# Reordering channels so that one matrix serves the group norms, and projecting q and k together: a four-layer fp32 convolution stack on one core

## The chip, the cores and the metric

The kernel runs on one core of one Trainium2 chip. The metric is device time in microseconds (us) of one execution; lower is better. The kernel before has a median of 4973.22 us over 3 runs (4967.2 to 4978.35). All data and all arithmetic are fp32.

## The reference, cut to what matters

The input x is 4 x 384 x 64 x 64 (batch, channels, height, width). Four layers follow, each as `x = x + layer(group_norm(x))`. A group norm has 32 groups, so 12 neighbouring channels share one mean and one variance per batch.

```python
def _gn(v, G=32, eps=1e-5):
    g = v.reshape(B_, G, C_ // G, H_, W_)
    m = jnp.mean(g, axis=(2, 3, 4), keepdims=True)
    s = jnp.var(g, axis=(2, 3, 4), keepdims=True)
    return ((g - m) / jnp.sqrt(s + eps)).reshape(v.shape)
...
# layer 0: attention on the first 96 channels, then a projection of all 384
xn = layer_norm_over_channels(x[:, :96])
qkv = bn(einsum(w_qkv, xn))              # 16 q, 16 k, 96 v channels
attn = softmax(q^T k * 16**-0.5)         # 4096 x 4096 per batch
y = bn(einsum(w_proj, relu(concat([v attn^T, x[:, 96:]]))))
```

Layer 1 is a 1x1 convolution, a filter over 8x8 patches in the frequency domain, a 3x3 depthwise convolution, a gated gelu and a 1x1 convolution. Layer 2 has 5x5 and 3x3 depthwise convolutions, gates, and an MLP from 384 to 768 to 384 channels with batch norms. Layer 3 is a 7x7 depthwise convolution whose kernels depend on the data. Which order the channels lie in matters to none of this as long as every weight that is indexed by channel lies in the same order, and the output is put back.

## The kernel before, in words

The 384 channels lie as three blocks `j` of 128 partitions. Channel c sits in block c // 128 on partition c % 128.

**Group norm.** Every norm starts from a mean and a variance per channel, kept as `[128, 3, ...]` (partition, block). The sum over a group goes across partitions, so it is a matmul with a constant matrix. Groups of 12 don't divide 128, and a group can straddle two blocks. So there are seven constant matrices `group[i, j]`, |i - j| < 2, loaded at the start (L238), and one sum over groups takes seven matmuls (`of_group` within `norm_of_groups`, L355 to L384, with one moving column each; `over_groups`, L561, with four). `norm_of_groups` sums twice: first the means (`gn_pg`), which VectorE copies to `gn_gm`; then VectorE forms (mean - group mean)^2 + variance (`gn_d`, L376 to L378), which is summed as `gn_pv`; ScalarE reads that from PSUM and takes Ln and Exp for the inverse root (`gn_r`). It is called 12 times: for x of each batch (`x_norm`), for the output of layer 0 (end of `attention`, L767), and for the output of layer 1 (end of `layer1`, L846). `group_means` and `factors` (layer 3) use `over_groups` once each.

**q, k, v.** `qkv` (L614) works through eight blocks of 512 pixels. Of each it centers 96 channels with a matmul (`ln_s`), gets the variance with another (`ln_v`), normalises to `ln_xn`, and then projects. `wq4` holds the 16 query columns four times, at columns 0, 32, 64 and 96 (`q_m`, L633), since the scores use four row groups of 32 partitions side by side. `wk4` holds the key columns four times as well (`k_m`, L639). ScalarE copies `q_m` to `q[i]` in one instruction (L634); a DMA on SP's queue then writes a row of shifts into it (L635). VectorE takes from `k_m` four pieces of 32 partitions x 128 columns, group g from partitions 32 g (L641). Four small matmuls make `v_m` (L645).

**The order of the work.** The first phase (`phase_a`) runs the attention of batch b and, beside it, other work: the norm of batch b+1's x, layer 1 of batch b-1, and the qkv of batch b+1. `side_by_side` (L529) draws pieces of the other work after each of the 64 attention steps, in proportion to estimated costs that the pieces yield. The final order on each engine, the semaphores and the PSUM slots come from the framework's scheduler. In this phase the PSUM tiles made with `pm` (tag "m") share two banks: `q_m`, `k_m`, `v_m`, `ln_s`, `ln_v`, `gn_pg`, `gn_pv`, and the tiles of layers 0 and 1. The scores have one tile of four banks, the attention output has two banks.

An attention step is four matmuls of scores on row groups (`sc_s`, L715), two Exp instructions on ScalarE (`probs`, L723), and four matmuls with v (`av`, L752). A matmul of the code becomes two instructions on TensorE.

The later phases are the depthwise convolutions of layer 2 (`phase_b`), its MLP (`phase_ef`), and layer 3 (`phase_g`).

Of the kernel before, what the change touches and what calls it, by code (L numbers as in the profile page):

```python
# [21 lines left out]
F32 = mybir.dt.float32  # L22
AF = mybir.ActivationFunctionType
ALU = mybir.AluOpType
AX = mybir.AxisListType

B, C, H, W = 4, 384, 64, 64
N = H * W
NJ = 3
P = 128  # L30
PD = 96
# [41 lines left out]
def _constants():  # L73
    parts = {}
    parts["ident"] = np.eye(P)
    center = np.zeros((P, PD))
    center[:PD] = np.eye(PD) - 1.0 / PD
    parts["center"] = center
    parts["mean96"] = np.full((P, PD), 1.0 / PD)
    group = np.arange(C) // (C // 32)  # L80
    same = (group[:, None] == group[None, :]) / (C // 32)
    for i in range(NJ):
        for j in range(NJ):
            if abs(i - j) < 2:
                parts[f"group{i}{j}"] = same[i * P : (i + 1) * P, j * P : (j + 1) * P]
    basis, pick = _fourier()

    inv = np.zeros((2, 64, 8, 2, 8))
    for p in range(2):
        inv[p, :, :, p, :] = basis.reshape(64, 8, 8)  # L90
    inv = inv.reshape(P, P)
    parts["to_coef"] = inv.T
    parts["to_pos"] = inv
    pick_t = np.zeros((P, P))
    pick_t[:40] = np.concatenate([pick.T, pick.T], axis=1)
    parts["pick"] = pick_t
    parts["mean384"] = np.full((P, P), 1.0 / C)

    e, x = np.arange(P) // W, np.arange(P) % W
    near = np.abs(x[:, None] - x[None, :]) <= 3  # L100
    parts["band7"] = near[:, 0:W]
    parts["cols7"] = near & (e[:, None] == e[None, :])
    parts["same32"] = np.tile(np.eye(32), (4, 4))
    net = np.zeros((P, 2 * P))
    net[0, :P] = 1.0
    net[1, P:] = 1.0
    net[2, P:] = -1.0
    parts["net"] = net
    at = 0
    for k, v in parts.items():  # L110
        _CONST_COLS[k] = (at, at + v.shape[1])
        at += v.shape[1]
    return np.concatenate(list(parts.values()), axis=1).astype(np.float32)

_HID = np.concatenate([np.arange(0, 128), np.arange(192, 320), np.arange(128, 192), np.arange(320, 384)])


def _cols(v):  # L120
# [38 lines left out]


def _layout(i):
    vec = {}
    for k in ("bn2_g", "bn2_b", "bn2_m", "bn2_v"):
        vec[k] = _cols(i[f"L0_conv_{k}"])
# [62 lines left out]
class _Builder:  # L227
    def __init__(self, ctx, tc, ins, out):
        self.ctx, self.tc, self.nc = ctx, tc, tc.nc
        self.ins, self.out = ins, out  # L230
        nc = self.nc
        self.keep = ctx.enter_context(tc.tile_pool(name="keep", bufs=1))
        self.small = ctx.enter_context(tc.tile_pool(name="small", bufs=2))
        self.dram = ctx.enter_context(tc.tile_pool(name="dram", bufs=1, space=bass.MemoryType.DRAM))
        self.vecs = self.keep.tile([P, ins["vecs"].shape[1]], F32, tag="vecs", name="vecs")
        nc.sync.dma_start(self.vecs, ins["vecs"])
        self.ident = self.const(self.keep, "ident")
        self.group = {  # L238
            (i, j): self.const(self.keep, f"group{i}{j}") for i in range(NJ) for j in range(NJ) if abs(i - j) < 2
        }  # L240
        self.eps = self.keep.tile([P, 1], F32, tag="eps", name="eps")
        nc.gpsimd.memset(self.eps, EPS)
        self.scratch = {
            k: [[self.dram.tile([P, N], F32, tag=f"{k}{b}{j}", name=f"{k}_{b}_{j}") for j in range(NJ)] for b in range(B)]
            for k in ("x2",)
        }

        self.tok = self.dram.tile([UNITS, B, 32, N], F32, tag="tok", name="tok")

        self.wx, self.h2 = (  # L250
            [self.dram.tile([P, NJ, N], F32, tag=f"{k}{b}", name=f"{k}_{b}") for b in range(B)] for k in ("wx", "h2")
        )


        self.rest = self.dram.tile([P, 32, B, P], F32, tag="rest", name="rest")
        self.raw = [self.dram.tile([P, P, P], F32, tag=f"raw{j}", name=f"raw_{j}") for j in range(NJ - 1)]
        self.shifts = [self.dram.tile([4, N], F32, tag=f"shift{b}", name=f"shift_{b}") for b in range(B)]

        self.xa, self.x1 = (
            [self.dram.tile([P, NJ, N], F32, tag=f"{k}{b}", name=f"{k}_{b}") for b in range(B)] for k in ("xa", "x1")  # L260
        )

        self.d53 = [
            [self.dram.tile([32, B, 32, P], F32, tag=f"d{i}{u}", name=f"d_{i}_{u}") for u in range(UNITS)]
            for i in range(2)
        ]
        self.hidden = [self.dram.tile([6, P, N], F32, tag=f"hid{b}", name=f"hid_{b}") for b in range(B)]

        self.norm2 = self.keep.tile([P, 3, NJ, B], F32, tag="norm2", name="norm2")
        self.r2, self.n2, self.p2 = (self.norm2[:, i] for i in range(3))  # L270
        self.mvt_ = self.keep.tile([P, 2, NJ, B], F32, tag="mvt", name="mvt")
        self.mvt = self.mvt_.rearrange("p k j b -> p j b k")
# [79 lines left out]
        a, c = self.bn_scale_shift(name, mv[:, 0:1], mv[:, 1:2], g, b)  # L352
        nc.scalar.activation(out, z, func, bias=c, scale=a)

    def norm_of_groups(self, mv, beside=False):  # L355


        nc = self.nc

        def of_group(name, src):  # L360
            out = self.pm(name)
            for j in range(NJ):
                near = [i for i in range(NJ) if abs(i - j) < 2]
                for i in near:
                    nc.tensor.matmul(
                        out[:, j : j + 1], lhsT=self.group[i, j], rhs=src(i), start=i == near[0], stop=i == near[-1]
                    )
            return out

        pg = of_group("gn_pg", lambda i: mv[:, i, 0:1])  # L370
        gm = self.sm([P, NJ], "gn_gm", 3)
        nc.vector.tensor_copy(gm, pg[:, 0:NJ])
        d = self.sm([P, NJ], "gn_d")

        mean = pg[:, 0:NJ] if beside else gm
        nc.vector.tensor_sub(d, mv[:, :, 0], mean)  # L376
        nc.vector.tensor_mul(d, d, d)
        nc.vector.tensor_add(d, d, mv[:, :, 1])  # L378
        pv = of_group("gn_pv", lambda i: d[:, i : i + 1])
        r = self.sm([P, NJ], "gn_r", 3)  # L380
        self.rsqrt(r, pv[:, 0:NJ])
        n = self.sm([P, NJ], "gn_n", 3)
        nc.vector.scalar_tensor_tensor(n, mean, -1.0, r, ALU.mult, ALU.mult)
        return r, gm, n, mv  # L384


    def qkv_weights(self, pool):
# [3 lines left out]
        nc = self.nc  # L391
# [24 lines left out]
        for g in range(4):  # L416
            nc.vector.tensor_copy(self.wq4[:, g, 1:17], wt[:, 0:16])
            nc.vector.tensor_copy(self.wk4[:, g, 1:17], wt[:, 16:32])
        nc.vector.tensor_copy(self.wv[:, 0:PD], wt[:, 32:P])
        self.score_bound(pool, wt)  # L420

    def score_bound(self, pool, wt):
# [191 lines left out]
    def qkv(self, b, q, k4, vt):  # L614
        nc = self.nc
# [7 lines left out]
        for i in range(8):  # L623
# [5 lines left out]
                yield 1.0  # L629
            xa = xn[i]  # L630
            q[i] = self.big.tile([P, 512], F32, tag="q", name="q", bufs=9)
            m = self.pm("q_m")
            nc.tensor.matmul(m, lhsT=self.wq4.rearrange("p g d -> p (g d)"), rhs=xa, start=True, stop=True)  # L633
            nc.scalar.copy(q[i], m)  # L634
            nc.sync.dma_start(  # L635
                q[i].rearrange("(g d) n -> g d n", g=4)[:, 0], self.shifts[b][:, i * 512 : (i + 1) * 512]
            )
            m = self.pm("k_m")
            nc.tensor.matmul(m, lhsT=self.wk4.rearrange("p g d -> p (g d)"), rhs=xa, start=True, stop=True)  # L639
            for g in range(4):  # L640
                nc.vector.tensor_copy(k4[32 * g : 32 * g + 32, i], m[32 * g : 32 * g + 32, g * P : (g + 1) * P])  # L641
            m = self.pm("v_m")
            mv = m.rearrange("p (c d) -> p c d", d=P)
            for c in range(4):
# [906 lines left out]
    def group_means(self):  # L1551

        nc = self.nc
        m = self.over_groups("gn_pg", self.mean2)
        nc.vector.tensor_copy(self.gm, m)
        for i, k in enumerate((-6.0, -7.0, 2.0)):
            nc.vector.tensor_scalar(self.off[:, :, :, i], self.gm, k, None, ALU.mult)
        nc.gpsimd.memset(self.s_s, 1.0)
        nc.vector.tensor_scalar(self.s_b, self.gm, -1.0, None, ALU.mult)

    def over_groups(self, name, v):

        m = self.pm(name)[:, 0 : NJ * B].rearrange("p (j b) -> p j b", b=B)
        for j in range(NJ):
            near = [i for i in range(NJ) if abs(i - j) < 2]
            for i in near:
                self.nc.tensor.matmul(
                    m[:, j], lhsT=self.group[i, j], rhs=v[:, i], start=i == near[0], stop=i == near[-1]
                )
        return m  # L1570

    def factors(self):

        nc = self.nc
# [5 lines left out]
        sq = tile_of("g_sq")  # L1580
        nc.vector.tensor_mul(sq, avg, avg)
        nc.vector.scalar_tensor_tensor(d, d, 1.0 / N, sq, ALU.mult, ALU.add)
        pv = self.over_groups("gn_pv", d)
        r = tile_of("g_r")
        self.rsqrt(r, pv)
        nc.vector.tensor_mul(avg, avg, r)
# [299 lines left out]
```

## Time and profile before

| | |
|---|---|
| median, 3 runs | 4973.22 us (4967.2 to 4978.35) |
| profiled execution, span of its instructions (the page gives no other time of it) | 4964.9 us |
| TensorE (PE) busy | 4552.7 us, 92%, 17665 matmul instructions |
| VectorE (DVE) busy | 2769.8 us, 56%, 4438 |
| ScalarE (ACT) busy | 2136.4 us, 43%, 2873 |
| GpSimd (POOL) busy | 777.5 us, 16%, 593 |
| mean granted TensorE clock | 0.962 |
| attention phase with its neighbours | about 62 to 2300 us |
| rest of layer 1, then layer 2's convolutions | about 2300 to 3170 us |
| layer 2's MLP | about 3195 to 4195 us |
| layer 3 | about 4200 to 4965 us |

"Busy" is the time in which an engine executes something. It is an average over stages. The row of tenths shows the span in 40 slices. A timeline line has start and duration in us, engine, line, operation, output and inputs, the number of instructions merged, and in brackets the idle time before it with what ended it. PEld is the load of the stationary operand, which runs beside the matmul before it.

### The profile page before, as it was taken

What the parts mean: (1) busy time and instruction counts of PE and PEld (TensorE: products, weight loads), DVE (VectorE), ACT (ScalarE), POOL (GpSimd) and SP (SyncE); (2) the same over time, 40 slices, a digit from 0 to 9 for tenths busy, and PEclk for the clock granted to TensorE, in tenths of its full rate; (3) what the DMA queues carried; (4) which work ended last, traced back from release to release, by engine and by line L of the source; (5) the groups of instructions that cost most, each with busy time, mean ns of one, the idle gap of its engine ahead of it and who ended that gap; (6) DMA issues with size and microseconds to landing.
All of it is one profiled execution on the core that took longest, in us unless ns stands there. A gap on an engine that the chain in (4) does not pass through costs nothing.

```text
span 4964.9 us, 47732 instructions
## 1 busy us (share of the span) xinstructions
PE 4552.7 (92%) x17665; PEld 2564.5 (52%) x17665; DVE 2769.8 (56%) x4438; ACT 2136.4 (43%) x2873; POOL 777.5 (16%) x593
## 2 busy tenths in 40 slices
PE   5999999999999999998989999699999998677988
PEld 2343444434443344444557888444444443577888
DVE  5322465644666445555867778655531112667898
ACT  4444344454444444444435666411123333764321
POOL 1000000000000000000025555100000001125554
PEclk9999999999999999998989999799999999699999
DMA  5210211211111111112338999776664443896776
GB/s 169 73 47 30 85 54 55 72 56 39 64 64 51 55 45 58 58 57 78 120 122 276 291 292 292 250 278 256 256 245 157 153 152 132 316 343 203 239 255 227
DMA packets 346710, 752.64 MB, mean 152 GB/s; under 512 B 22779, under 2 KB 173158, under 8 KB 337510
## 3 DMA queue, kind: packets, MB, share of 16 engines
q1 hardware_dynamic: 280728, 475.46, 30.1%
q0 software_dynamic: 32640, 151.28, 7.9%
q10 hardware_dynamic: 33102, 122.77, 6.3%
q8 instruction: 143, 2.34, 0.2%
q14 instruction: 97, 0.79, 0.0%
HBM read 447.16 MB, written 302.25 MB: 151 GB/s over the span
## 4 chain that ended last, share of the span: by engine, by line
PE 45%; DVE 9%; DMA 4%; ACT 3%; issue 3%; POOL 1%; SPq 0%; ACTq 0%; DVEq 0%; POOLq 0%
PE h_s L1380 10%; PE h_m L1432 10%; PE conv_m L1156 9%; PE av L752 3%; PE t_m L871 2%; PE conv_m L1757 2%; DVE acc L948 2%; DMA wmix<-in_mix_t 1%; DMA g_h<-h 1%; PE out_m L966 1%; PE proj_m L785 1%; PE sc_s L715 1%; DVE toep L1744 1%; PE taps_m L941 1%; DVE toep L1137 1%
## 5 line engine op out<-in xcount | busy, mean ns | idle before, releaser
L752 PE MATMUL av<-probs,vt 128*128 128x512 f32 x2048 | 965.6, 607 | 0.0
L723 ACT ACTIVATE probs<-sc_s 128x1024 f32<-128x1024 f32 x512 | 500.9, 1021 | 789.8 <-PE av L752 783.7
L752 PEld LDWEIGHTS av<-probs,vt 128*128 128x128 f32 x2048 | 371.7, 192 | 468.1 <-issue 461.0
L1156 PE MATMUL conv_m<-toep,z 128*128 128x256 f32 x2304 | 519.4, 385 | 10.6 <-DVE toep L1137 5.1
L948 DVE SCALAR_TENSOR_TENSOR acc<-band,vecs,acc 128x512 f32<-128x512 f32 x708 | 496.9, 747 | 45.7 <-POOL band L909 39.9
L1432 PE MATMUL h_m<-f_h,cm_w_t 128*128 128x512 f32 x1152 | 496.7, 595 | 8.7 <-ACT f_h L1422 8.7
L1156 PEld LDWEIGHTS conv_m<-toep,z 128*128 128x128 f32 x2304 | 439.4, 193 | 71.0 <-DVE z L1089 4.9
L1757 PE MATMUL conv_m<-toep,z 128*128 128x128 f32 x3072 | 392.8, 286 | 42.1 <-DVE toep L1744 19.2
L1757 PEld LDWEIGHTS conv_m<-toep,z 128*128 128x128 f32 x3072 | 378.7, 202 | 44.4 <-POOL toep L1744 18.2
L1380 PE MATMUL h_s<-e_tok,cm_w_t 128*128 128x512 f32 x768 | 363.4, 596 | 5.5 <-DVE e_tok L1365 5.5
L1137 POOL TENSOR_TENSOR toep<-w,band 128x1536 f32<-128x1536 f32 x94 | 324.0, 3447 | 278.0 <-PE conv_m L1156 232.0
L1432 PEld LDWEIGHTS h_m<-f_h,cm_w_t 128*128 128x128 f32 x1152 | 220.0, 191 | 285.4 <-issue 273.3
L715 PE MATMUL sc_s<-q,k 32*128 32x512 f32 x2048 | 296.3, 647 | 21.9 <-ACT probs L723 21.4
L1440 DVE BATCH_NORM_STATS2 h_st<-f_h 128x6 f32<-128x512 f32 x96 | 66.4, 694 | 429.1 <-ACT f_h L1439 429.1
L871 PE MATMUL t_m<-w_in_t,xb 128*128 128x384 f32 x768 | 276.7, 495 | 3.4 <-DVE coef L888 2.1
L1387 ACT COPY e_h<-h_s 128x1024 f32<-128x1024 f32 x96 | 97.2, 1012 | 401.5 <-PE h_s L1380 401.5
L785 PE MATMUL proj_m<-xm,w_proj_t 128*128 128x512 f32 x576 | 265.2, 599 | 4.6 <-DVE xm L738 3.5
L792 DVE SCALAR_TENSOR_TENSOR x_res<-proj_m,bn_c,x_res 128x512 f32<-128x512 f32 x96 | 71.8, 748 | 319.0 <-PE proj_m L785 315.9
L1380 PEld LDWEIGHTS h_s<-e_tok,cm_w_t 128*128 128x128 f32 x768 | 147.0, 192 | 189.5 <-issue 183.2
L1389 DVE BATCH_NORM_STATS2 h_st<-e_h 128x6 f32<-128x512 f32 x192 | 123.4, 685 | 202.8 <-ACT e_h L1387 202.8
L871 PEld LDWEIGHTS t_m<-w_in_t,xb 128*128 128x128 f32 x768 | 142.9, 192 | 139.0 <-issue 59.3
L1380 PE MATMUL h_s<-z,cm_w_t 128*128 128x512 f32 x384 | 196.2, 593 | 0.0
(380 smaller groups left out, 6206.2 us busy)
## 6 DMA issues: line engine op xcount, KB each, us to landing
d<-d_o ACTq DMA_DIRECT2D x96, 512.0 KB
c_d<-d SPq DMA_DIRECT2D x96, 512.0 KB
hid<-e_h ACTq DMA_DIRECT2D x16, 3072.0 KB
f_h<-hid SPq DMA_DIRECT2D x16, 3072.0 KB
x_in<-in_x SPq DMA_DIRECT2D x96, 256.0 KB
x_res<-in_x SPq DMA_DIRECT2D x32, 768.0 KB
xa<-x_res POOLq DMA_DIRECT2D x32, 768.0 KB, 3.9
xa_in<-xa SPq DMA_DIRECT2D x32, 768.0 KB
```

The source lines that it names most:

```text
L715: nc.tensor.matmul(s[:, g], lhsT=k4[32 * g : 32 * g + 32, c], rhs=q[i][32 * g : 32 * g + 32], start=True, stop=True,)
L723: nc.scalar.activation(p[:, h * 1024 : (h + 1) * 1024], s[:, 2 * h : 2 * h + 2].rearrange("p a b -> p (a b)"), AF.Exp, scale=0.25,)
L752: nc.tensor.matmul(av, lhsT=vt[:, 4 * c + v, :], rhs=p[:, v * 512 : (v + 1) * 512], start=c == 0 and v == 0, stop=c == 7 and v == 3,)
L785: nc.tensor.matmul(m, lhsT=self.w_proj[:, j, o * P : (o + 1) * P], rhs=xm[:, j], start=j == 0, stop=j == NJ - 1,)
L871: nc.tensor.matmul(m[:, 0:C], lhsT=xb[:, j], rhs=self.w_in[:, j, :], start=j == 0, stop=j == NJ - 1,)
L948: nc.vector.scalar_tensor_tensor(out, src(j, k), w, done, ALU.mult, ALU.add)
L1137: eng.tensor_tensor(t, self.w53[:, at : at + 192].rearrange("p (m n) -> p m n", n=8).unsqueeze(2).to_broadcast([P, 24, 8, 8]), band.rearra ...
L1156: nc.tensor.matmul(m[:, c * 256 : (c + 1) * 256], lhsT=self.z_[:, at : at + P], rhs=t[:, 12 * c + 4 * i : 12 * c + 4 * i + 4].rearrange("p ...
L1380: nc.tensor.matmul(s[:, v, :], lhsT=w1[:, j, o * P : (o + 1) * P], rhs=t[j][:, v * 512 : (v + 1) * 512], start=j == 0, stop=j == NJ - 1,)
L1389: nc.vector.bn_stats(st[:, o, 8 * b + 2 * i + v, :], h[:, o, v * 512 : (v + 1) * 512])
L1432: nc.tensor.matmul(m, lhsT=w2[:, o, j * P : (j + 1) * P], rhs=h[:, o, v * 512 : (v + 1) * 512], start=o == 0, stop=o == 5,)
L1757: nc.tensor.matmul(m[:, ch * P : (ch + 1) * P], lhsT=self.z_[:, at : at + P], rhs=t[:, 8 * c + 2 * i : 8 * c + 2 * i + 2].rearrange("p m a ...
```

## The change

The channels are permuted on the host. Block j now holds, on its partitions 0 to 95, eight whole groups (channels 0 to 95, 192 to 287 and 288 to 383), and on partitions 96 to 127 the j-th third of each of the eight groups of channels 96 to 191, four channels of each. Then one matrix `group` describes every block: twelve neighbouring partitions belong together below 96, four above. The first 96 channels stay on block 0's first 96 partitions, where the attention wants them. All weights indexed by channel are permuted on the host, and so is the output.

One sum over groups is now one matmul with all blocks as moving columns, into an `m` of PSUM. VectorE then copies partitions 0 to 95, adds the three blocks for partitions 96 to 127, and copies that sum to all three blocks.

For q and k, `wqk` has the query columns at 0, 32 and 64 and the key columns at 96. One matmul gives `qk_m`. ScalarE copies partitions 0 to 95 to q, and with a second instruction partitions 64 to 95 to q's partitions 96 to 127. VectorE takes all four pieces of k from partitions 96 to 127.

```diff
-        self.group = {
-            (i, j): self.const(self.keep, f"group{i}{j}") for i in range(NJ) for j in range(NJ) if abs(i - j) < 2
-        }
+        self.group = self.const(self.keep, "group")
...
+    def of_groups(self, name, v):
+        nc = self.nc
+        n = v.shape[2]
+        m = self.pm(name)[:, 0 : NJ * n].rearrange("p (j n) -> p j n", n=n)
+        nc.tensor.matmul(m, lhsT=self.group, rhs=v, start=True, stop=True)
+        out = self.sm([P, NJ, n], f"{name}_{n}", 3)
+        nc.vector.tensor_copy(out[0:PD], m[0:PD])
+        s = self.sm([P, n], f"{name}_{n}s")
+        nc.vector.tensor_reduce(s[PD:P], m[PD:P].rearrange("p j n -> p n j"), AX.X, ALU.add)
+        nc.vector.tensor_copy(out[PD:P], s[PD:P].unsqueeze(1).to_broadcast([P - PD, NJ, n]))
+        return out
...
-        pg = of_group("gn_pg", lambda i: mv[:, i, 0:1])
-        gm = self.sm([P, NJ], "gn_gm", 3)
-        nc.vector.tensor_copy(gm, pg[:, 0:NJ])
+        gm = self.of_groups("gn_pg", mv[:, :, 0:1])[:, :, 0]
...
-        pv = of_group("gn_pv", lambda i: d[:, i : i + 1])
+        pv = self.of_groups("gn_pv", d)[:, :, 0]
         r = self.sm([P, NJ], "gn_r", 3)
-        self.rsqrt(r, pv[:, 0:NJ])
+        self.rsqrt(r, pv)
...
+        self.wqk = pool.tile([PD + 1, 4, 32], F32, tag="wqk", name="wqk")
+        nc.vector.tensor_copy(self.wqk[:, 0:3], self.wq4[:, 0:3])
+        nc.vector.tensor_copy(self.wqk[:, 3], self.wk4[:, 3])
...
-            m = self.pm("q_m")
-            nc.tensor.matmul(m, lhsT=self.wq4.rearrange("p g d -> p (g d)"), rhs=xa, start=True, stop=True)
-            nc.scalar.copy(q[i], m)
+            m = self.pm("qk_m")
+            nc.tensor.matmul(m, lhsT=self.wqk.rearrange("p g d -> p (g d)"), rhs=xa, start=True, stop=True)
+            nc.scalar.copy(q[i][0:96], m[0:96])
+            nc.scalar.copy(q[i][96:128], m[64:96])
...
-            m = self.pm("k_m")
-            nc.tensor.matmul(m, lhsT=self.wk4.rearrange("p g d -> p (g d)"), rhs=xa, start=True, stop=True)
             for g in range(4):
-                nc.vector.tensor_copy(k4[32 * g : 32 * g + 32, i], m[32 * g : 32 * g + 32, g * P : (g + 1) * P])
+                nc.vector.tensor_copy(k4[32 * g : 32 * g + 32, i], m[96:128, g * P : (g + 1) * P])
...
-        m = self.over_groups("gn_pg", self.mean2)
+        m = self.of_groups("g_pg", self.mean2)
...
-        pv = self.over_groups("gn_pv", d)
+        pv = self.of_groups("g_pv", d)
```

The rest of the diff is on the host: the permutation `_ORDER`, the list of weights it applies to, and its inverse on the output.

## The prediction

> **What bounds the kernel now.** I read the row of busy tenths first. From the second slice to the nineteenth (one slice is 124 us, so to about 2300 us) TensorE is at 9, and VectorE, ScalarE and DMA are not.
>
> ```profile
> PE   5999999999999999998989999699999998677988
> DVE  5322465644666445555867778655531112667898
> ACT  4444344454444444444435666411123333764321
> ```
>
> Everything that the change removes lies in this stretch, except the start and two sums in layer 3. A busy TensorE need not be the limit, so I read the chain of waits of a piece of it. From 1760 to 1790 us it holds TensorE alone, back to back: 14 `av` instructions in 6.01 us, 0.429 us each.
>
> ```profile
> 1767.24 1.07 PE sc_s L715 x8
> 1768.31 0.86 PE back_m L896 x6
> 1769.18 6.01 PE av L752 x14
> ```
>
> The engine's waits between 600 and 900 us come to 3.6 us in 300. So there a microsecond taken off TensorE is one taken off the time. The start is different. Of 60 to 140 us TensorE idles about 20, and the timeline shows why:
>
> ```profile
> 95.60 0.68 ACT L314 ACTIVATE ln_rs<-ln_v,eps 96x512 f32<-96x512 f32 x1
> 96.33 1.13 PE L639 MATMUL k_m<-ln_xn,wk 97*128 97x512 f32 x2 [1.35 <-ACT ln_rs L314]
> 98.13 0.56 ACT L634 COPY q<-q_m 128x512 f32<-128x512 f32 x1
> 98.74 1.16 PE L645 MATMUL v_m<-wv,ln_xn 97*128 97x128 f32 x8 [0.42 <-ACT q L634]
> 100.19 1.07 PE L589 MATMUL ln_s<-ln_x,center 96*96 96x512 f32 x2 [0.29 <-DVE k L641]
> ```
>
> Each tile of the two-bank pool waits until the tile two before it is read: `k_m` for `ln_v`, `v_m` for `q_m`, the next `ln_s` for `k_m`. ScalarE's strict order (Ln, table, Exp, then the q copy) sets the beat, about 10 us a block.
>
> **The norms**, from the timeline, once inside attention and once where attention ends:
>
> ```profile
> 1740.36 0.16 DVE L372 COPY gn_gm<-gn_pg 128x3 f32<-128x3 f32 x1 [2.15 <-PE gn_pg L365]
> 1740.56 0.16 DVE L376 TENSOR_TENSOR gn_d<-gn_mv,gn_gm 128x3 f32<-128x3 f32 x1
> 1741.17 1.72 PE L365 MATMUL gn_pv<-gn_d,group 128*128 128x1 f32 x14
> 2280.45 2.56 PE L365 MATMUL gn_pv<-gn_d,group 128*128 128x1 f32 x14 [0.84 <-DVE gn_d L378]
> 2286.86 3.42 PE L365 MATMUL gn_pg<-gn_mv,group 128*128 128x1 f32 x14
> 2291.13 3.15 PE L365 MATMUL gn_pv<-gn_d,group 128*128 128x1 f32 x14 [0.84 <-DVE gn_d L378]
> ```
>
> Fourteen instructions with one moving column take 1.72 us at full clock (0.123 each) and up to 3.4 us when the clock has fallen. Dependent VectorE operations start 0.2 us apart.
>
> **What the Trainium skill says.** "TensorE: Matmul & The Clock Gate", section LDWEIGHTS: the load's time goes by the 128 columns of the stationary operand (by its formula about 107 ns). The trace agrees: 0.123 us per instruction with a single moving column, so fewer matmuls, not smaller ones, save here. Same page, "The HAM clock gate": an idle TensorE falls to half clock; the trace has 0.225 us per instruction at 2291 us. "PSUM — Partial Sum Buffer", section on bank collisions: two engines may not touch one bank in the same 32-partition quadrant at once, different quadrants may. `qk_m` is read by ScalarE (partitions 0 to 95) and VectorE (96 to 127), different quadrants; whether the framework still puts one after the other no run here shows, since before no such tile has two readers at once. I carry both ends.
>
> **The change, part by part.**
>
> *(1) The k projection.* 32 matmuls go, two instructions of 0.429 us each: 0.86 us per block. 24 of them lie inside attention (batches 1 to 3), where the chain is TensorE: 24 x 0.86 = 20.6 us. Against it, `qk_m` holds one of the two banks until two ScalarE copies (the trace gives 32x512 and 128x512 at L774 and L778 the same 806 ns, so the second costs a full 0.57 us) and four VectorE copies (4 x 0.286) are through. Side by side the hold is 1.15 us, like `k_m`'s now; in sequence about 2.4 us plus queueing. On ScalarE an Exp pair (1.94 us) is queued behind the extra copy, and `sc_s` waits for it; an Exp pair now starts after 2 to 5 us of idleness, which covers 0.57 us. SP's shift DMA comes 0.57 us later, and behind it loads of x; the scores that need q are a batch away. I take 5 us of stall over the 24 (bounds 0 and 20): gain **15**, bounds 0 and 21.
>
> *(2) The same for batch 0, at the start.* Four pool tiles per block in place of five; `v_m` no longer waits for q's copy but takes `k_m`'s place (2.4 us earlier in the lines above); the next `ln_s` waits for `qk_m`, about when it started before (q copy end 98.7 + 0.57 + k's copies 1.2 = 100.4 in sequence, 99.3 side by side). The gain per block is 0 to 1.2 us, with +0.57 on ScalarE's beat against it. I take 0.5 x 8 = **4**, bounds -4 and 10.
>
> *(3) Norms inside attention.* Eight of the twelve (x of batches 1 to 3, layer 0 of batches 0 to 2, layer 1 of batches 0 and 1). Each sum falls from 14 to 2 instructions, 12 x 0.12 = 1.4 us; 16 sums give 22 us. VectorE's chain grows: before `gn_d` by two operations (0.4 us), after `gn_pv` by three (0.6, and a semaphore, 0.75). TensorE stands in order behind the first: 8 x 0.4 = 3 us where no other matmul fills it. The second lengthens only the way to `gn_r`, and that starts 1.4 earlier. Gain **18**, bounds 8 and 22.
>
> *(4) The end of attention, 2276 to 2294 us.* Two norms in series on a slowed TensorE: 2.56 + 3.42 + 3.15 us before `t_m` can start become about 3 x 0.4; the last piece of the first `gn_pg` gives 0.4; the VectorE chains cost 2 x 0.4. That is 7.5; `xb` on ScalarE, which `t_m` also needs, limits it. I take **6**, bounds 2 and 8. Layer 1's last norm (2531 to 2540 us) lies beside the store and reload of its last band, which the chain of waits names there: 0.
>
> *(5) The start.* SP issues six loads less, at 3.65 us for seven: loads of x go out 3.1 us sooner. But VectorE begins the statistics of x at 16.0 us, behind the preparation of the weights, and is then busy to 32 us; two more copies for `wqk` cost 0.3. ScalarE's waits for earlier DMAs may shift by either sign: **1**, bounds -1 and 4. The first norm, on a slow TensorE and alone: its two sums of 3.1 us become about 0.5 (the first overlaps the last statistics, so 1.5 + 2.6) against 1.15 on VectorE: **3**, bounds 2 and 4.
>
> *(6) Layer 3.* `group_means` falls from 3.1 to about 0.5 us, with three VectorE operations more. The chain there is the load of `g_h`, landing at 4208, and `gm` is ready at 4203.5: 0. `factors`: 1.6 us of TensorE against three operations of VectorE in a queue with 1.22 us `toep` operations; 0, bounds -2 and 2.
>
> The host's permutation and equally shaped DRAM tensors cost nothing on the device. Later phases issue the same instructions.
>
> Sum: 15 + 4 + 18 + 6 + 1 + 3 = **47 us**. All of it lies inside the profiled span of 4964.9, which becomes 4918. The median lies 8.3 us above that span; I carry this over: 4973.2 - 47 = **4926 us**. The sum of all lower bounds is a gain of 5 (0 - 4 + 8 + 2 + 1 - 2), that of all upper ones 71.
>
> **The rivals.**
>
> *A, the saving is half handed on.* The two-bank pool turns the shorter TensorE stream into waits for `qk_m`, and the VectorE steps of the norms sit behind 0.75 us `acc` operations. For: VectorE's queue delayed k's copies at 1749 us by 2.5 us, and `t_m` waited 1.05 for them. Against: only such single waits. Parts (1) to (3) then give 3 + 0 + 8, the total about 20: 4953 us.
>
> *B, slower: `qk_m` blocks the pool.* Should an Exp pair (1.94 us) and a table load (1.28) stand between ScalarE's two copies, and VectorE's copies wait for both, the bank is held 3 to 5 us more, and VectorE's queue stops with it. For: ScalarE's order is strict and the beat at the start is already its. Against: both copies are traced together. It decides when the stall passes (47 + 5) / 32 = 1.6 us a block, over what (1) charges; at 2.4 us a block it costs 77 us against the 52 gained: about 4998 us.
>
> *C, more.* The bank comes free early, each block's beat at the start falls by 2 us (16 in all), and every other part reaches its upper bound: 21 + 16 + 22 + 8 + 4 + 4 + 2 = 77, so 4896 us. For: the start's order on ScalarE leaves room. Against: it needs every part to go well.
>
> *D, no change:* gains and stalls cancel, at a stall between A's and B's: 4973 us. That the change doesn't do what it says I exclude: twelve partitions below 96 and 3 x 4 above are just the groups, with the same divisor.
>
> **How the numbers follow.** Likeliest case 0.62, with 4903 to 4948 as its own range; A 0.16 (4948 to 4963); B 0.09; C 0.08 (4880 to 4903); D 0.05. Range 4896 to 4962: the first case whole, A nearly, half of C, about 0.8. Within 0.2% (10 us, what a measurement of this kernel can tell from none) is D, 0.05; faster is 0.62 + 0.16 + 0.08 = 0.86; slower is B, 0.09.
>
> **What would show it.** TensorE's matmul instructions fall by 64 + 288 + 24 = 376, to about 17289; ScalarE's rise by 32; VectorE's by 68. Right for (1): `v_m` follows `qk_m` after 0.9 us, and TensorE's waits on `qk_m`'s readers stay below 0.3 us a block. Right for (3): `gn_pv` is 2 instructions in about 0.3 us, `gn_d` 0.4 us later after its matmul. Right for (4): `t_m` of the last batch starts about 6 us sooner relative to the end of `proj_m`. Rival A or B shows as new TensorE waits for L641 or for the q copies, or as `sc_s` waiting longer for `probs` than the 21.4 us now. The prediction would also be wrong if the scheduler's new order changed stages that hold none of these instructions.

## The result, and the profile after

The changed kernel takes 4923.20 us (median of 4 runs, 4915.61 to 4930.93), beside 4974.24 us for the kernel before in the same series. The ratio is 0.9897, 95% interval [0.9883, 0.9911]: 51 us less, inside the predicted range and 3 us from the predicted 4926. The profiled execution took 4921.93 us with a span of 4920.2 us. As will be seen, two errors of opposite sign hide in that agreement.

The page of the changed kernel, its first line of busy times and the rows of tenths that answer to those shown of before:

```profile
PE 4484.3 (91%) x17289; PEld 2510.4 (51%) x17289; DVE 2787.8 (57%) x4506; ACT 2155.9 (44%) x2905; POOL 777.6 (16%) x593
...
PE   5999999999999999999978999699999997678988
...
DVE  5322566645656345565867778555521113667898
ACT  5444444555445544445245666311123334753321
```

TensorE issues 17289 matmul instructions, 376 fewer, as counted; ScalarE 32 more, VectorE 68 more. TensorE's busy time is 68.4 us smaller, the time only 51, so not every microsecond taken off TensorE shortened the whole. Attention is still TensorE's. Its waits from 600 to 900 us, by cause (us in total, times, longest), still add up to 3.6 us:

```profile
PE back_m L936 <- ACT t_t L919: 2.3, 2, 1.5
PE coef_m L926 <- DVE x_res L832: 0.7, 2, 0.5
PE sc_s L755 <- ACT probs L763: 0.6, 3, 0.2
```

The start's timeline, one block of the projections:

```profile
84.84 1.02 PE L674 MATMUL qk_m<-ln_xn,wqk 97*128 97x512 f32 x2
85.56 0.68 ACT L354 ACTIVATE ln_rs<-ln_v,eps 96x512 f32<-96x512 f32 x1
...
86.29 1.16 PE L685 MATMUL v_m<-wv,ln_xn 97*128 97x128 f32 x8 [0.43 <-ACT ln_rs L354]
...
88.09 0.56 ACT L675 COPY q<-qk_m 96x512 f32<-96x512 f32 x1
...
88.66 0.58 ACT L676 COPY q<-qk_m 32x512 f32<-32x512 f32 x1
...
89.53 1.22 DVE L681 COPY k<-qk_m 32x128 f32<-32x128 f32 x4
```

`v_m` has taken `k_m`'s place behind `ln_rs` and waits for no copy of q. The second copy of q costs as much as the first, with a third of the partitions. The copies of k come after it, although they read other partitions (96 to 127, where ScalarE reads 64 to 95). So the hold of `qk_m` is the long one of the prediction's two: from the start of the first copy to the end of the last it is 2.7 us in this block and 2.4 to 4.8 over all 32. TensorE hardly feels it. The tile view of `qk_m`, who waited for its readers and its matmul (us, times):

```profile
who waited for it (us, times):
  ACT q L675: 15.8, 8
  DVE k L681: 4.4, 7
  PEld proj_m L825: 3.0, 2
  PE proj_m L825: 2.1, 4
  PEld sc_s L755: 0.8, 1
  PE ln_v L642: 0.5, 2
```

TensorE itself waits 2.6 us in all 32 blocks together. A norm inside attention (timeline):

```profile
1690.40 0.28 PE L400 MATMUL gn_pg<-gn_mv,group 128*128 128x3 f32 x2
...
1690.72 0.16 DVE L402 COPY gn_pg<-gn_pg 96x3 f32<-96x3 f32 x1 [0.81 <-PE gn_pg L400]
1690.89 0.17 DVE L404 TENSOR_REDUCE gn_pg_1s<-gn_pg 32x1 f32<-32x3 f32 x1
1691.09 0.17 DVE L405 COPY gn_pg<-gn_pg_1s 32x3 f32<-32x3 f32 x1
1691.29 0.16 DVE L414 TENSOR_TENSOR gn_d<-gn_mv,gn_pg 128x3 f32<-128x3 f32 x1
...
1693.51 0.39 PE L400 MATMUL gn_pv<-gn_d,group 128*128 128x3 f32 x2
```

A sum is 0.28 to 0.39 us on TensorE, not 1.72, and the two added VectorE steps cost 0.4 us, 0.2 apart. The end of attention, TensorE's timeline:

```profile
2225.53 0.39 PE L400 MATMUL gn_pg<-gn_mv,group 128*128 128x3 f32 x2 [1.98 <-DVE gn_mv L596]
2227.13 0.39 PE L400 MATMUL gn_pv<-gn_d,group 128*128 128x3 f32 x2 [1.22 <-DVE gn_d L416]
...
2232.97 0.56 PE L400 MATMUL gn_pg<-gn_mv,group 128*128 128x3 f32 x2 [2.00 <-DVE gn_mv L596]
2234.75 0.59 PE L400 MATMUL gn_pv<-gn_d,group 128*128 128x3 f32 x2 [1.22 <-DVE gn_d L416]
2235.20 5.55 PE L911 MATMUL t_m<-w_in_t,xb 128*128 128x384 f32 x12
```

The waits for `gn_d` grew from 0.84 to 1.22 us, the sums shrank from 2.56, 3.42 and 3.15 us to 0.4 to 0.6.

**Where the time came from.** I take events that exist in both traces and compare when they come. The executions of the kernel before scatter (the first profile, span 4964.9, lay at the lower end), so I use a second profile of it (the run `e4_before_again`, span 4970.8), which lies near the median, beside the first of the changed kernel:

| stretch | before | after | gain | predicted |
|---|---|---|---|---|
| start to the last step of the first norm (`gn_n`) | 40.66 | 35.07 | 5.6 | 4 |
| to the copies of k of batch 0's last block | 94.6 | 86.3 | 8.3 | 4 |
| attention, to the last norm of layer 0 | 2151.6 | 2110.2 | 41.4 | 33 |
| to the last norm of layer 1 | 254.7 | 250.0 | 4.7 | 6 |
| layer 2, the MLP, first part of layer 3 | 1753.6 | 1755.1 | -1.5 | 0 |
| first matmul of layer 3's convolution to the end | 675.6 | 683.5 | -7.9 | 0 |
| sum | 4970.8 | 4920.2 | 50.6 | 47 |

Up to 2500 us the kernel gains 60 us, 13 more than predicted. Layer 3 then gives 8 back. These are single profiles: in attention two more of the changed kernel gain 39.8 and 38.8 us, not 41.4.

### The profile page after: what moved, and what is told of

Same layout as the page of the kernel before. It is cut to its first block, busy times and chain, and to the rows that moved or that the text cites. A ratio compares the mean times of both kernels' runs of the same rounds, so it can differ in the third digit from the quotient of the medians.

```text
span 4920.2 us, 47066 instructions
## 1 busy us (share of the span) xinstructions
PE 4484.3 (91%) x17289; PEld 2510.4 (51%) x17289; DVE 2787.8 (57%) x4506; ACT 2155.9 (44%) x2905; POOL 777.6 (16%) x593
## 4 chain that ended last, share of the span: by engine, by line
PE 67%; DVE 13%; ACT 8%; DMA 7%; issue 4%; POOL 1%; SPq 0%; ACTq 0%; DVEq 0%; POOLq 0%
PE av L792 14%; PE h_s L1420 10%; PE h_m L1472 9%; PE conv_m L1196 9%; PE sc_s L755 5%; PE proj_m L825 4%; PE t_m L911 3%; DVE acc L988 3%; PE out_m L1006 2%; PE conv_m L1786 2%; PE out_m L1005 2%; PE back_m L936 2%; DMA wmix<-in_mix_t 1%; ACT probs L763 1%; DMA g_h<-h 1%
## 5 line engine op out<-in xcount | busy, mean ns | idle before, releaser
L1786 PE MATMUL conv_m<-toep,z 128*128 128x128 f32 x3072 | 391.4, 285 | 40.5 <-POOL toep L1773 21.6
```

The source lines that it names most:

```text
L1786: nc.tensor.matmul(m[:, ch * P : (ch + 1) * P], lhsT=self.z_[:, at : at + P], rhs=t[:, 8 * c + 2 * i : 8 * c + 2 * i + 2].rearrange("p m a ...
```

## The experiments

**The two halves alone.** My theory: the norms give about 30 us, the joint projection 24 to 30, and they add. Rival: both shorten TensorE's stream in attention, so that part of one is lost when the other is there. `e1_norms_only` has the permuted channels and the one matrix, with q and k projected apart:

```diff
-            m = self.pm("qk_m")
-            nc.tensor.matmul(m, lhsT=self.wqk...)
-            nc.scalar.copy(q[i][0:96], m[0:96])
-            nc.scalar.copy(q[i][96:128], m[64:96])
+            m = self.pm("q_m")
+            nc.tensor.matmul(m, lhsT=self.wq4...)
+            nc.scalar.copy(q[i], m)
...
+            m = self.pm("k_m")
+            nc.tensor.matmul(m, lhsT=self.wk4...)
...
```

> The new channel order and the one-matrix sums over groups, but q and k projected apart as before. The parts add (theory 1): the start with the first norm 6 us (the changed kernel's trace is 5.96 us ahead when gn_n of the first norm is written), eight norms in attention 18 (8 to 22), the end of attention 6: together about 30, so 4944 us. Rival (the norms' saving is handed to VectorE's longer chain): under 15 us, so above 4959. In the stages after attention theory 1 expects the same lengths as before (586 us from the first to the last conv_m of layer 2, 475 us from the second sum of layer 3 to the end); if the change itself lengthened them by 4 and 7 us, as the changed kernel's one profile shows, this kernel shows it as well, since it has the new sums there.

`e2_qk_only` is the kernel before with the opposite edit: q and k from one matrix (`wqk`), the sums over groups as they were.

> The kernel before with the joint q and k projection alone; channel order, seven matrices and sums over groups as before. Theory 1: the projections of batch 0 give 9 us (the changed kernel gains that between gn_n of the first norm and the end of batch 0's k), those of batches 1 to 3 give 15 to 21 us: together 24 to 30, so 4944 to 4950 us. Rival (the bank held by qk_m turns the saving into waits): under 12 us, above 4962, with new TensorE waits on the copies of k or q. The stages after attention have nothing changed and should have the lengths of before within the scatter.

The changed kernel and the kernel before ran once more beside them.

> The changed kernel unaltered, for a second profile and more times: 4923 us (4915 to 4931). If the longer last stages (590 us for layer 2's convolutions against 586, 482 us for the end of layer 3 against 475) come from the change, they stand in this profile too within 2 us; if they are scatter from one execution to the next, they move by several us.

> The kernel before unaltered, for a second profile: 4974 us. If the last stages scatter, 586 us (layer 2's convolutions) and 475 us (end of layer 3) move by several us here; if they don't, they stand within 2 us, and the 11 us that the changed kernel loses there come from the change.

| kernel | median us (range) | ratio to before, 95% interval | lead at the last norm of layer 1 |
|---|---|---|---|
| norms only | 4948.53 (4944.65 to 4959.96) | 0.9955 [0.9938, 0.9973] | 31.2 |
| joint projection only | 4939.77 (4931.62 to 4949.22) | 0.9930 [0.9915, 0.9946] | 27.4 |
| both (the changed kernel) | 4929.04 (4922.14 to 4932.41) | 0.9908 [0.9888, 0.9928] | 58.9 |
| before | 4972.95 (4964.61 to 4979.24) | 1.0001 [0.9990, 1.0012] | 0 |

At the end of layer 1 the leads add: 31.2 + 27.4 = 58.6, beside 58.9. The rival finds no support, though each lead is from one profile and can't tell a few microseconds from none. The start's 8 to 10 us of the projections belong to the joint projection alone (84.2 us from the first norm to the last block's copies of k, against 93.7 with the norms alone). At the end they don't add: 24 and 33 us, but 44 together (51 in the first series), and the norms alone have lost 7 of their 31. Something that comes with the norms costs time after attention.

**Does ScalarE's second copy set the beat of the start?** It costs 0.576 us, 32 times. `e7_q_copy_on_dve` gives it to VectorE:

```diff
-            nc.scalar.copy(q[i][96:128], m[64:96])
+            nc.vector.tensor_copy(q[i][96:128], m[64:96])
```

> The changed kernel with q's fourth part (32 partitions) copied by VectorE in place of ScalarE. If ScalarE's second copy (0.576 us, 32 times) sets the beat at the start, batch 0 of the projections (from the first norm to the last copy of k, 86.3 and 85.2 us) shortens by 2 to 4.6 us, and the kernel takes 2 to 5 us less. If the copies of k, which follow all others of the bank, set it, the piece only changes its place in that series: start within 1 us, time within 2 us. If VectorE's queue delays q, attention lengthens: up to 24 x 0.3 = 7 us more.

It takes 4940.67 us (4932.69 to 4946.23) beside 4924.89 us of the changed kernel on the same chip, 16 us more; none of the three expectations was that large. The tile view of its `qk_m`: the copy's durations (min, median, max in ns), and from "who waited for it" the two readers.

```profile
L676 DVE COPY q<-qk_m x32: 690/690/691, 60.0 to 1706.8; 32x512 f32<-32x512 f32 x32
...
  DVE q L676: 27.4, 16
  ACT q L675: 20.1, 8
```

VectorE's copy of q now waits for ScalarE's: 27.4 us of an idle VectorE, where k's copies idled 4.4. Batch 0's projections take 91.0 us in place of 84.5 in the neighbouring profile of the changed kernel, and the way from the first norm to the last norm of layer 0 takes 12 us more in all (2209.3 against 2197.3; this profile is the fastest of its six executions). The extra work is on the right engine as it is.

**Loads or matmuls at the start?** `e8_six_loads` puts six loads that nothing reads back on SyncE:

```diff
         self.group = self.const(self.keep, "group")
+        for i in range(6):
+            t = self.keep.tile([P, P if i else 32], F32, tag=f"idle{i}", name=f"idle{i}")
+            nc.sync.dma_start(t, ins["consts"][:, 0 : t.shape[1]])
```

> The changed kernel with six loads of constants that nothing reads (five of 128x128, one of 128x32) put back on SyncE ahead of the loads of x. If the earlier loads of x gave the start its gain, SyncE starts them near 7.5 us, not 4.0, and the first norm's gn_n moves from 34.7 to 35.1 us to 37 to 38.5. If the smaller matmuls gave it all, gn_n stays within 0.5 us. Time: 0 to 4 us over the changed kernel's.

SyncE starts the loads of x at 8.24 us, not 4.02, VectorE the statistics of x at 15.71 us, not 8.20, and `gn_n` comes at 37.50 us, not 34.70 to 35.20: 2.3 to 2.8 us later. The share of the two sums is the firmer one. From the first mean and variance (`gn_mv`) to `gn_n` it is 9.41 us in the kernel before and 6.46 in the changed one, with the idle loads too: 2.95 us. That the rest is the loads' is likely, but one profile can't show it, since two profiles of one program (`e5_late_matmul` and `e11_late_matmul_again`, below) have `gn_n` at 34.21 and 36.68 us. The time, 4925.05 us (4922.08 to 4927.56), can't tell 2 us from none.

**The loss in layer 3.** The scheduler orders layer 3 differently in the changed kernel, from `factors` on; in the norms-only version too, but not in the one with the joint projection alone. `factors` on the kernel before (timeline, PE, DVE and ACT):

```profile
4488.21 1.62 PE L1567 MATMUL gn_pv<-g_d,group 128*128 128x4 f32 x14
4489.69 2.25 PE L1757 MATMUL conv_m<-toep,z 128*128 128x128 f32 x18
4489.87 0.27 ACT L314 ACTIVATE g_r<-gn_pv,eps 128x12 f32<-128x12 f32 x1 [2.88 <-PE gn_pv L1567]
...
4491.69 0.17 DVE L1586 TENSOR_TENSOR g_avg<-g_avg,g_r 128x12 f32<-128x12 f32 x1 [5.17 <-ACT g_r L315]
...
4491.92 0.39 PE L1593 MATMUL xw_m<-g_avg,w_gate 128*128 128x4 f32 x2
4491.98 1.01 ACT L1766 COPY rest_o<-conv_m 128x1024 f32<-128x1024 f32 x1 [0.32 <-PE conv_m L1757]
```

and on the changed kernel:

```profile
4436.27 0.29 PE L400 MATMUL g_pv<-g_d,group 128*128 128x12 f32 x2
4436.41 2.25 PE L1786 MATMUL conv_m<-toep,z 128*128 128x128 f32 x18
...
4436.98 1.12 DVE L1616 TENSOR_TENSOR g_max<-g_max,gm 128x12 f32<-128x12 f32 x1
4438.13 0.16 DVE L405 COPY g_pv<-g_pv_4s 32x12 f32<-32x12 f32 x1
4438.32 0.30 ACT L354 ACTIVATE g_r<-g_pv,eps 128x12 f32<-128x12 f32 x1 [2.07 <-DVE g_pv L405]
4438.70 1.01 ACT L1795 COPY rest_o<-conv_m 128x1024 f32<-128x1024 f32 x1
...
4441.02 0.21 ACT L355 ACTIVATE g_r<-g_r 128x12 f32<-128x12 f32 x1
...
4441.27 0.17 DVE L1615 TENSOR_TENSOR g_avg<-g_avg,g_r 128x12 f32<-128x12 f32 x1 [1.43 <-ACT g_r L355]
...
4441.50 0.39 PE L1622 MATMUL xw_m<-g_avg,w_gate 128*128 128x4 f32 x2 [2.83 <-DVE g_avg L1615]
```

Before, the 14 matmuls of the sum and 18 of the convolution cover the way over ScalarE exactly: `xw_m` starts without a wait. After, TensorE has 1.3 us less to do and the way from the sum to `g_avg` is 1.5 us longer (5.0 us, not 3.5). VectorE's steps lie on it, with an operation that had slipped between them, but they don't set its length. ScalarE does. Its copy `rest_o` takes the result of these 18 matmuls and starts 0.03 us after the last of them. Before, it came after both instructions of `g_r` (Ln, then Exp); now it stands between them, and a table load of 1.28 us comes after it. In the six profiles with the changed kernel's sums and its joint projection the Ln starts 1.36 to 2.17 us after the sum, but the Exp at 4.76 in each. So TensorE stands still for 2.83 us. Behind `xw_m` it then has 16 matmuls of the convolution until `gx_m`, where it had 26, and waits 3.6 us there.

The clock goes down beside them: it is 0.51 from 4443 to 4448 us and stays at a half to about 4460, and the 36 instructions of `xw_m` take 6.4 us in place of 4.2. Two window rows (start and end, length, then busy us and instructions of PE, PEld, DVE, ACT, POOL; clock, DMA share, GB/s), of before 6 to 12 us behind `g_avg`,

```profile
4497.70:4500.70 3.00, 3.00 (x18) 2.84 (x17) 3.00 (x7) 0.17 (x1) 1.55 (x2) 0.65 0.96 404
4500.70:4503.70 3.00, 2.11 (x18) 1.83 (x17) 2.99 (x6) 0.81 (x4) 2.32 (x3) 1.00 0.07 27
```

and of after, 6 to 9 and 15 to 18 us behind it:

```profile
4447.30:4450.30 3.00, 3.00 (x15) 3.00 (x16) 1.51 (x4) 0.21 (x1) 1.36 (x1) 0.50 0.72 306
...
4456.30:4459.30 3.00, 3.00 (x16) 3.00 (x16) 1.92 (x4) 0.90 (x2) 0.92 (x3) 0.50 0.00 0
```

The window row from the first `g_avg` to the end, before:

```profile
4491.70:4964.90 473.20, 401.92 (x3315) 389.31 (x3313) 412.73 (x461) 136.52 (x257) 240.30 (x162) 0.96 0.69 225
```

and after:

```profile
4441.30:4920.20 478.90, 407.86 (x3312) 395.31 (x3312) 415.46 (x460) 135.64 (x256) 239.30 (x161) 0.94 0.71 223
```

The 5.7 us that are lost in this piece are TensorE's busy time (5.9 us more for the same matmuls), at a lower clock; idle time is the same (71.3 and 71.0 us). Part of that is scatter: the second profile of before has 407.60 us busy in 475.30, at 0.95. The Trainium skill's page "TensorE: Matmul & The Clock Gate" (Part 1: The HAM clock gate) has half clock as the default, which activity releases, decided in free-running windows of about 3.4 us. The traces agree: summing what is missing to full clock, in slices of 3 us from `g_avg` on until the clock is back at 1.00 to stay for 9 us, I get 3.4 us of half clock in the first profile of before and 6.8 in the second, and 17.1 us in the changed kernel, whole multiples of 3.4. The kernel before has a dip there too, with no wait at `xw_m`. That the waits keep TensorE from leaving it is my reading and not shown: in the kernel before TensorE was busy for only 0.81 of the 3 us from 4509.7 us, and the clock stayed at 1.00.

Theory 1: the longer chain in `factors`, and the order that comes with it, cost the late time. Theory 2: scatter between executions, which the two profiles of before show too (layer 2's convolutions took 585.4 us in one and 590.8 in the other). `e5_late_matmul` takes the VectorE steps away in layer 3 alone:

```diff
+    parts["tail"] = parts["group"] * (np.arange(P) >= PD)[:, None]
...
+    def over_groups(self, name, v):
+        m = self.pm(name)[:, 0 : NJ * B].rearrange("p (j b) -> p j b", b=B)
+        for j in range(NJ):
+            near = [j] + [i for i in range(NJ) if i != j]
+            for i in near:
+                self.nc.tensor.matmul(m[:, j], lhsT=self.group if i == j else self.tail,
+                                      rhs=v[:, i], start=i == near[0], stop=i == near[-1])
+        return m
...
-        m = self.of_groups("g_pg", self.mean2)
+        m = self.over_groups("gn_pg", self.mean2)
...
-        pv = self.of_groups("g_pv", d)
+        pv = self.over_groups("gn_pv", d)
```

> The changed kernel, but with the two sums over groups of layer 3 (group_means and factors) made by matmuls alone and read from PSUM: nine small matmuls (own column with the block matrix, the two other columns with its last 32 rows) in place of one matmul and three VectorE operations. TensorE, VectorE, ScalarE and GpSimd then issue layer 3 in the order of the kernel before. Theory 1, the 10 us that the changed kernel gives back after attention come from the new order around factors: the stretch from g_avg (after g_r) to the end falls from 478.9 and 480.1 us to 473 to 475, and the kernel takes about 5 us less than the changed one, 4918 to 4922 us. Theory 2, they are scatter between executions and the late state of the chip: that stretch stays at 476 to 480 us and the time within 2 us of the changed kernel's.

> The changed kernel once more, beside the other three on the same chip. 4923 to 4930 us; the last norm of attention's end (gn_n11) at 2481 to 2483 us, the stretch from g_avg to the end 478 to 481 us if the late loss belongs to the kernel, 473 to 481 if it is scatter.

It takes 4912.37 us (4907.0 to 4919.75), ratio 0.9884 [0.9867, 0.9901], beside 4924.89 us (4923.0 to 4928.82), ratio 0.9907 [0.9892, 0.9922], of the changed kernel: 12.5 us less, with ranges apart. But the two profiles, 16.3 us apart, give theory 1 only 6.2 us: from the convolution's first matmul to the end 678.1 us against 684.3, of which the stretch behind `g_avg` has 477.1 against 479.6. The rest is mostly a lead of 9.6 us that it has already at the end of layer 0 (2222.95 against 2232.52), where the two versions hold the same instructions, but for one more load at the start and one operation on x moved. So I asked three things. Does the long chain do the same to the kernel before? `e9_before_plus_steps` changes nothing but:

```diff
         pv = self.over_groups("gn_pv", d)
+        for i in range(3):
+            e = tile_of(f"g_e{i}")
+            nc.vector.tensor_copy(e, pv)
+            pv = e
```

and the same three copies behind the sum in `group_means`.

> The kernel before, with three more VectorE copies of 128x12 behind each of the two sums over groups of layer 3; nothing else. All engines then issue layer 3 in the changed kernel's order, in a kernel whose attention is that of before. If the longer chain in factors costs the late 6 us, the stretch from the first conv7 matmul to the end grows from 675.7 us (two profiles of before) to 681 to 685, TensorE shows waits of about 3 us each at xw_m and gx_m, and the time is 5 to 8 us over the kernel before's. If the late loss is scatter, the time is within 2 us of the kernel before's.

Does the early lead come with the load? `e10_one_load` is the changed kernel with one idle load as in `e8_six_loads`:

> The changed kernel with one 128x128 load of constants that nothing reads on SyncE ahead of the loads of x. Up to layer 3 it has the instructions and the order of the version with layer 3's sums by matmuls (one statistics operation of x changes its place in VectorE's order). If that version's lead of 9 us at the end of attention (gn_n9 at 2222.95, not 2231.6 to 2233.6 us) comes from this start, gn_n9 is at 2221 to 2226 us here, and the time about 6 us over that version's, 4917 to 4920 us. If it was scatter, gn_n9 is at 2230 to 2234 and the time that of the changed kernel, 4923 to 4928 us.

And does the lead stay?

> The version with layer 3's sums by matmuls once more, beside the other two. If its lead over the changed kernel is its own, 4908 to 4916 us, first conv7 matmul to end 676 to 680 us, gn_n9 at 2221 to 2226 us. If the first time was luck, 4918 to 4926 us.

| kernel | median us (range) | ratio to before, 95% interval | convolution of layer 3 to the end |
|---|---|---|---|
| before + VectorE steps | 4982.43 (4972.05 to 4995.35) | 1.0024 [1.0017, 1.0030] | 686.4 |
| before, same series | 4970.92 (4964.76 to 4978.11) | | 675.8 and 675.6 in its two profiles |
| changed + one load | 4927.77 (4921.15 to 4928.41) | 0.9905 [0.9890, 0.9920] | 687.6 |
| layer 3's sums by matmuls, again | 4921.51 (4904.63 to 4922.23) | 0.9897 [0.9882, 0.9912] | 674.4 |

The first row settles that the VectorE steps, with the order that the scheduler makes for them, are enough for the loss: six small copies, 0.17 us each, cost the kernel before 11.5 us (8 to 15 by the interval), and the stretch grew by 10.7, both more than I had expected. TensorE's waits there, from 4180 us on,

```profile
PE gx_m L1619 <- DVE gx_n L1616: 3.6, 1, 3.6
...
PE xw_m L1601 <- DVE g_avg L1594: 2.8, 1, 2.8
```

are those of the changed kernel to the tenth. The 14 matmuls of the sum are still there, so the lost cover is not needed for the wait. What it shares with the changed kernel is the order: `rest_o` between the two instructions of `g_r`, and 16 matmuls ahead of `gx_m`. Its window row from `g_avg` to the end has the lower clock again:

```profile
4497.80:4978.50 480.70, 411.92 (x3312) 400.16 (x3312) 417.12 (x460) 135.53 (x256) 239.08 (x161) 0.93 0.70 221
```

With the sums by matmuls the row of the second run is close to that of before (the first run has 406.98 us busy in 477.10, at 0.94):

```profile
4429.60:4902.90 473.30, 403.52 (x3315) 391.05 (x3313) 412.68 (x461) 136.78 (x257) 240.28 (x162) 0.96 0.71 227
```

All profiles together: the eight with the VectorE steps in `factors` have `rest_o` inside `g_r`, both waits, 17.1 or 20.5 us of half clock behind `g_avg`, and 680.1 to 687.6 us from the convolution's first matmul to the end. The five without have `rest_o` behind `g_r`, no wait at `xw_m` and at most 0.9 us at `gx_m`, 3.4 or 6.8 us of half clock before TensorE is back at full speed, and 674.4 to 680.2 us. At the edge the two sets meet (the joint projection alone has 680.2), for there is scatter of 4 to 5 us as well. TensorE's busy time from `g_avg` to the end is 407.7 to 411.9 us in the eight and 401.9 to 407.6 in the five.

The early lead is not settled. The load alone doesn't bring it (the last norm of layer 0 at 2231.05 us), while the second profile of the matmul version has it again (2224.24). But three of that version's four executions in the second series took 4921.47 to 4922.23 us, so it is probably not there in each of them. The two versions differ before layer 3 in nothing that I can name as a cause.

The matmul version has the lower median in both series: by 12.5 us against the changed kernel, with ranges apart, and by 6.3 against the changed kernel with the idle load, with ranges that overlap. What of this is layer 3's is read from the stretches above, not from these medians, since the early lead is in them too.

## Why the prediction was right

It was right in sign and mechanism up to 2500 us, where it was 13 us short, and a late loss that I had put at nothing took most of these 13 back. That the total came within 3 us is luck.

*(1) The k projection in attention: 15 predicted (0 to 21).* With the joint projection alone the lead grows by 19.2 us from the copies of k of batch 0's last block to the last norm of layer 0. The 20.6 us of matmuls were right; the term that was mis-sized is the stall, 5 us, where TensorE waits 2.6 us for the readers of `qk_m` in all 32 blocks. The question that I left open, whether the framework serialises the two readers, has the answer yes: in all 32 blocks the copies of k start after q's second copy has ended, and seven times the trace has VectorE idle until then. The Trainium skill's page "PSUM — Partial Sum Buffer" (PSUM bank collisions) says that the compiler adds a dependency between engines for one bank and quadrant; here the order stands between different quadrants too. It costs little, since TensorE had other matmuls to run meanwhile. I had expected `v_m` 0.9 us behind `qk_m`; it is 0.86 to 3.70 us, 1.05 in the middle.

*(2) Batch 0: 4 predicted (-4 to 10), 8.3 to 10.7 measured* over the profiles, about the 1.2 us a block that I had as the upper end. I took 0.5 a block for the risk that ScalarE's 0.57 us would lengthen the beat; the measured gain leaves no room for that.

*(3) The norms in attention: 18 predicted.* With the norms alone the stretch to the last norm of layer 0 shortens by 17.4 us, of which 2.7 lie behind the start of the last `proj_m` and belong to (4): 14.7, inside the bounds. Its steps came as said: 0.28 to 0.39 us for a sum, 0.4 us more on VectorE.

*(4) The end of attention: 6 predicted, 5.7 measured:* from the start of the last `proj_m` to `t_m` 27.3 us became 21.6 (2213.55 to 2235.20), with the sums at 0.4 to 0.6 us as worked out and a wait of 1.22 in place of 0.84 us. The table above cuts this stretch in two at the last norm of layer 0. With (1) and (3) its first part makes 36.6 us of that row's 38.8 to 41.4; the rest I can't place. The kernel before and `e9_before_plus_steps`, the same up to layer 3, differ by 4 us there (2151.4 and 2151.6 against 2147.5).

*(5) The start: 4 predicted, 5.5 to 6.3 measured.* The sums are worth 3, as said. The loads were put at 1, since I thought that VectorE's preparation of the weights holds the statistics of x back in any case. It doesn't: they begin at 8.2 us, not 16.0, and their first `gn_mv` comes 2.5 to 3.4 us earlier.

*(6) Layer 3: 0 predicted (-2 to 2), -7.6 to -9.6 measured* over three profiles of the changed kernel, from the convolution's first matmul on. This step failed. In `factors` I set 1.6 us of matmuls against three short operations in VectorE's queue, took them to cancel, and left everything else in its place. The queue that counted was ScalarE's, where the scheduler's new order put `rest_o`, which waits for the convolution, into the middle of `g_r`. `xw_m` then waits 2.83 us and `gx_m` 3.6, and TensorE is at half clock for 17 us or more. The missing matmuls, which were cover for the way over ScalarE, count as well. An estimate from the traces: with the Exp 1.58 us behind the Ln, as before, `xw_m` would still wait 1.0 to 1.8 us. How much of the loss is the waits, how much the order of what lies behind them and how much the clock wasn't separated: adding or taking away the VectorE steps moved all of it at once, and no run put `rest_o` alone back in its place. Of the signs that the prediction named, one comes near ("the scheduler's new order changed stages that hold none of these instructions"), but the loss begins in a stage that does hold them, and no price stood beside it.

*The frame of the sum.* The 8.3 us between span and median do not lie around the span. Time and span differ by 1.7 to 1.8 us in each profile that has both (4921.93 and 4920.2 in the first of the changed kernel), so the other 6.6 most likely say that this execution of before was quicker than its median. The gain in us was subtracted from the median, so the forecast didn't suffer.

Of the rivals, A and B fall with the waits on `qk_m`, 0.08 us a block. C had 2 us a block at the start and every other part at its upper bound; the block came out at 1.0 to 1.3 us, and even up to 2500 us the gain was 60 of its 77. D, no change, falls with the 51 us.

## What to carry to other kernels

Here a matmul instruction cost about 0.12 us whether it had one moving column or four (14 in 1.72 us and in 1.62), so a layout that turns fourteen of them into two was worth 1.3 to 1.4 us each time TensorE was the bound. Where TensorE only bridges a wait, the same edit can turn round. Look in the timeline at the whole way that the result takes over the other engines, and at what the new order puts into each of their queues: a copy that waits for other work, between two halves of a short chain, set the length of the way here, and not the steps that were added. Count the slower clock after the gap too. Where one stage loses, keep the old form there: the version with matmuls in layer 3 and the one matrix everywhere else has the lowest medians of all that ran.

## What the runs showed of the hardware

Six VectorE copies of 12 columns, 1.0 us of work, cost 11.5 us in a kernel of 4971, in the order that the scheduler made for them, with two waits of 2.8 and 3.6 us and 20.5 us of half clock where there had been 3.4 to 6.8. A copy from PSUM of 32 x 512 took 0.576 us on ScalarE and 0.690 on VectorE, 96 x 512 took 0.569 on ScalarE: the number of partitions made no difference. Executions of the same instructions in the same order differ by more than 5 us in single stages (layer 2's convolutions: 585.4 and 590.8 us in two profiles of the kernel before, 590.4 to 593.1 in three of the changed one), so a single profile doesn't place a loss of that size.
